# A fourth mask buffer, two residual buffers loaded later, and the first batch's input in halves

## The chip, the cores and the metric

The kernel runs on one core of one Trainium2 chip. The metric is the device time of one execution in microseconds (us). The time before is the median of seven runs, 2154.57 us (2151.7 to 2155.99). One execution was recorded by the hardware profiler; all readings of the profile are from that one, and times in it count from the start of its span.

The engines have short names in the profile: PE is TensorE (its matmuls; PEld its loads of weights), DVE is VectorE, ACT is ScalarE, POOL is GpSimd, and SP is SyncE, whose queue (SPq) issues most of the transfers.

## What is computed

One layer of a network on 32 graphs (batches) of 512 nodes with 256 features each, all in float32. Cut to what matters:

```python
h = relu(layernorm(x))                        # x: (32, 512, 256), over the features
xc = h.transpose(0, 2, 1)
c = relu(bn1(conv1d(xc, conv1_w)))            # one tap
c = bn2(conv1d(c, conv2_w, pad=8))            # 17 taps along the nodes
x_conv = relu(c + xc).transpose(0, 2, 1)
s = h @ w_se.T + b_se                         # three numbers per node
A = exp(-squared_distances(s)) * adj          # adj: (32, 512, 512), the mask
x_nmp = A @ relu(h @ w_msg.T + b_msg)
# a GRU cell, input [x_conv, x_nmp], state h
gi = concat(x_conv, x_nmp) @ w_ih.T + b_ih
gh = h @ w_hh.T + b_hh
r, z = sigmoid(gi_r + gh_r), sigmoid(gi_z + gh_z)
n = tanh(gi_n + r * gh_n)
out = x + (1 - z) * n + z * h                 # x: the layer's input, the residual
```

## The kernel before

**Streams.** Five streams of work are written as Python generators (line 1068): `rows` (layer norm and transposition of the first four batches, and the one-tap convolution of all), `begins` (the same preparation of the later batches), `graphs` (messages, distances, masking and the sum over neighbours), `conv` (the 17-tap convolution, four batches at a time, as 25 products of transformed inputs and transformed weights), and `gates` (the GRU cell and the output). A loop (line 1106) always takes the next piece of the stream that is furthest behind.

**A planner with a clock of its own.** The order of each engine's instructions is fixed while the program is built. `now` is an estimated time of PE, and every `matmul` or `turn` (a transposition on PE) adds to it. `Engine` (line 107) keeps an estimated `free` time for DVE and ACT: a fixed cost per instruction plus one per element. A generator yields the time from which its next piece may go. After each piece `fill` (line 1027) puts background work on DVE as long as `dve.free < now + 1.5`: layer norms of later batches (`norm_some`), the convolution's operands, transformed weights and sums. `later` (line 144) keeps short follow-up pieces until their time has come. So where a step yields, and what the estimate of `dve.free` is, can alter the written order of everything behind it.

**Layer norm.** `fetch` (line 161) loads 512 x 256 numbers as one transfer into a tile of 128 partitions by four chunks. `norm` (line 274) is a generator. For each chunk DVE makes statistics and aggregates them, and it yields after every second chunk; then `rsqrt` (line 212) adds epsilon on DVE and raises to the power -0.5 on POOL for all four chunks at once; then DVE makes the shifts, and ACT applies scale and shift to each chunk in place. For batch 0 the whole generator is run at once before the loop (line 1080), since nothing else can be done yet. PE then transposes the normed chunks (`norm_t`, line 309), and `conv1` (line 321) follows.

**Masks.** The 512 x 512 mask of a batch is four tiles of 128 rows, `m_sb`, with three buffers. `masked` (line 741) takes one tile: for the first eight batches PE transposes it into a PSUM bank (`ps_g`, of which there are three) and DVE multiplies it into `at`; for the others DVE transposes and multiplies. Then `gr.ask(1)` asks for one mask more. As the buffers are given out in turn, that is the mask three places on: the first three masks of a batch are asked for while the batch before is masked, and the fourth when the first of its own batch has been used. `gather` (line 756) then multiplies `at` with the messages.

**Residual.** At the end of a gate half (`o` is 0 or 1, half of the features), `leave` (line 911) transposes the result on DVE and adds `XR[b, o]`, the tile `res` with the layer's input in blocks of 32 x 32; `store` (line 918) writes it out from POOL's queue in four transfers. `load_res` (line 776) issues four transfers of 64 KB on SP's queue. `res` has three buffers. The two tiles of batch 0 are loaded after the first update of batch 0 (line 973), each later one when the tile of the same half of the batch before has been stored (line 928), two half-batches ahead.

**Gates.** `gates` (line 861) goes for each `o` through the products of r, of the hidden part, of z and of n. Their evacuations are `reset` (a sigmoid on ACT into `r`; before it `settle` writes out all pieces still kept by `later`, the store of the half before among them), `reset_hidden`, `update` (a sigmoid on ACT into `z`) and `mix`.

**When the gates start.** `late_pools` (line 686) opens the memory of the late stage when the first group's last product comes; there `whh` and `wih`, the GRU's weights (768 and 1536 KB), are loaded on SP's queue.

SP issues its transfers strictly in the written order; each waits for its buffer, and those behind it wait too.

Of the kernel before, what the change touches and what calls it, by code (L numbers as in the profile page):

```python
# [8 lines left out]
F32 = mybir.dt.float32  # L9
AF = mybir.ActivationFunctionType  # L10
ALU = mybir.AluOpType
PSUM = bass.MemoryType.PSUM

P = 128
# [21 lines left out]
TURNED = 8  # L36
# [8 lines left out]
def kernel(  # L45
# [28 lines left out]
    nc = tc.nc  # L74
    B, N, D = x.shape
    NT = N // P
    ND = D // P
# [8 lines left out]
    front = ctx.enter_context(tc.tile_pool(name="front", bufs=2))  # L86
# [7 lines left out]
    late = None  # L94
# [4 lines left out]
    LAG = 0.6  # L99
# [22 lines left out]
    dve, act = Engine(nc.vector, 0.12, 0.00108), Engine(nc.scalar, 0.16, 0.0009)  # L122
# [21 lines left out]
    def later(t, f):  # L144
        LATER.append((t, f))
        LATER.sort(key=lambda e: e[0])

    def settle():
        while LATER:
            LATER.pop(0)[1]()  # L150


    XS, HT, HB, HR, HG, XN, XR = {}, {}, {}, {}, {}, {}, {}
# [6 lines left out]

    def fetch(b, xs=None):
        XS[b] = front.tile([P, NT, D], F32, name="x_sb", bufs=2) if xs is None else xs
        nc.sync.dma_start(XS[b], x[b].rearrange("(c p) d -> p c d", p=P))

    def load(b, xs=None):
        if b not in XS:
# [13 lines left out]
    def load_gates(b):  # L180
        if b >= B or b in HB:
            return
        HB[b] = late.tile([P, ND, N], F32, name="hTb", bufs=2)
        nc.sync.dma_start(HB[b], HD[b])

    def load_sums(b, d):
        if b < B and (b, d) not in XN:
            XN[b, d] = late.tile([P, N], F32, name="xnb", bufs=2)
            nc.sync.dma_start(XN[b, d], ND_[b, d])
# [22 lines left out]
    def rsqrt(dst, var):  # L212

        n = dst.shape[-1]
        t = front.tile([P, 4], F32, name="veps")
        dve.tensor_scalar(t[:, :n], var, EPS, None, op0=ALU.add)
        nc.gpsimd.tensor_tensor(dst, t[:, :n], mhalf[:, :n], op=ALU.pow)
# [19 lines left out]
    class Graphs:  # L237
# [15 lines left out]
        def ask(self, more):  # L253

            for k in range(self.asked, min(self.asked + more, NT * B)):
                b, c = k // NT, k % NT
                m = self.masks[b, c] = front.tile([P, N], F32, name="m_sb", bufs=3)
                rows = adj[b].rearrange("(k i) m -> i k m", i=32)  # L260
                if b < TURNED:
                    nc.sync.dma_start(m, adj[b, c * P : (c + 1) * P, :])
                for g in range(P // 32 if b >= TURNED else 0):
                    at = c * P + 32 * g
                    nc.sync.dma_start(
                        m[32 * g : 32 * g + 32, :].rearrange("i (k j) -> i k j", j=32),
                        rows[:, :, at : at + 32],
                    )
                self.asked = k + 1

    gr = Graphs()


    def norm(b):

        xs = XS[b]
        st = front.tile([P, NT, 6], F32, name="st")
        mv = front.tile([P, NT, 2], F32, name="mv")
        for c in range(NT):
            dve.bn_stats(st[:, c, :], xs[:, c, :])  # L280
            dve.bn_aggr(mv[:, c, :], st[:, c, :])
            if c % 2:
                yield 0.0
        rstd = front.tile([P, NT], F32, name="rstd")
        rsqrt(rstd, mv[:, :, 1])
        yield dve.free + 2.0
        shift = front.tile([P, NT], F32, name="shift")
        dve.scalar_tensor_tensor(
            shift, mv[:, :, 0], -1.0, rstd, op0=ALU.mult, op1=ALU.mult
        )  # L290
        yield dve.free + 0.2
        for c in range(NT):
            act.activation(
                xs[:, c, :], xs[:, c, :], AF.Identity if b < TURNED else AF.Relu, bias=shift[:, c : c + 1],
                scale=rstd[:, c : c + 1],
            )
            if c % 2:
                yield act.free + LAG

    def norm_some(b):  # L300

# [284 lines left out]
    def all_operands():  # L586
        for _ in range(NG):
            yield from operands()

    xs = all_operands()  # L590
# [177 lines left out]
    def blocks(t, rows, o):  # L768
        for g in range(P // 32):
            at = o * P + 32 * g  # L770
            nc.sync.dma_start(
                t[32 * g : 32 * g + 32, :].rearrange("i (k j) -> i k j", j=32),
                rows[:, :, at : at + 32],
            )

    def load_res(b, o):
        if b < B and (b, o) not in XR:
            XR[b, o] = late.tile([P, N], F32, name="res", bufs=3)
            blocks(XR[b, o], XB[b], o)


# [79 lines left out]
    def gates(b):  # L861
# [33 lines left out]
        def mix_next(r, z, o, s):  # L895
            act.activation(
                r[:, s], r[:, s], AF.Tanh,
                bias=vec[:, _COL["b_ih"] + 2 * ND + o : _COL["b_ih"] + 2 * ND + o + 1],
            )
            later(act.free + 0.3, lambda: mix_last(r, z, o, s))  # L900
# [17 lines left out]
        def store(y, o, s):  # L918
            for g in range(P // 32):
                at = slice(32 * g, 32 * g + 32)  # L920
                queue = nc.gpsimd if s.stop - s.start == N else nc.scalar if g % 2 else nc.sync
                queue.dma_start(  # L922
                    OB[b][:, s.start // 32 : s.stop // 32, o * P + 32 * g : o * P + 32 * g + 32],
                    y[at, s].rearrange("i (k j) -> i k j", j=32),
                )
            if s.stop == N:
                del XR[b, o]
                load_res(b + 1, o)

        for o in range(ND):  # L930
            r = z = None

            def reset():
                nonlocal r
                settle()
                r = late.tile([P, N], F32, name="r", bufs=2)
                act.activation(r, ps_r, AF.Sigmoid, bias=brz[:, o : o + 1])

            def reset_hidden():
                dve.scalar_tensor_tensor(  # L940
                    r, ps_h, vec[:, _COL["b_hh"] + 2 * ND + o : _COL["b_hh"] + 2 * ND + o + 1], r,
                    op0=ALU.add, op1=ALU.mult,
                )

            def update():
                nonlocal z
                z = late.tile([P, N], F32, name="z")
                act.activation(z, ps_z, AF.Sigmoid, bias=brz[:, ND + o : ND + o + 1])

            def mix(s=slice(0, N)):  # L950
                dve.tensor_tensor(r[:, s], ps_n[:, s], r[:, s], op=ALU.add)
                later(dve.free + 0.3, lambda r=r, z=z, o=o: mix_next(r, z, o, s))
                if o == ND - 1:
                    load_sums(b + 1, 0)
                    load_sums(b + 1, 1)

            ps_r = acc.tile([P, N], F32, name="ps_acc")
            if o == 0:
                yield lambda: b in evacuated
                yield evacuated[b]  # L960
                yield from residual()
                yield from products(ps_r, o, 0, 0, 1, (0, 2))
                yield act.free + LAG
            else:
                yield from products(ps_r, o, 0, 0, 1, (0, 2))
            yield from products(ps_r, o, 0, 1, 3, (0, 2), reset)
            ps_h = acc.tile([P, N], F32, name="ps_acc")
            yield from products(ps_h, o, 2, 0, 1, (0, 0), reset_hidden)
            ps_z = acc.tile([P, N], F32, name="ps_acc")
            yield from products(ps_z, o, 1, 0, 3, (0, 2), update)  # L970
            if o == 0:
                load_gates(b + 1)
                for k in range(ND if b == 0 else 0):
                    load_res(0, k)
            ps_n = acc.tile([P, N], F32, name="ps_acc")
            if b < B - 1 or o < ND - 1:
                yield from products(ps_n, o, 2, 1, 3, (1, 2), mix)
                continue

            for h in range(2):  # L980
                s = slice(h * N // 2, (h + 1) * N // 2)
                if h > 0:
                    ps_n = acc.tile([P, N], F32, name="ps_acc")
                for j in range(2 * ND):
                    matmul(
                        ps_n[:, s], wih[:, j, cols(o, 2)], x_in[j][:, s],
                        start=(j == 0), stop=(j == 2 * ND - 1),
                    )
                mix(s)
                yield now  # L990
            settle()
# [109 lines left out]
    for c in range(ND):  # L1101
        for k0, k1 in ((0, 9), (9, TAPS)):
            nc.sync.dma_start(wflat[:, c, k0 + 1 : k1 + 1, :], conv2_w[:, c, k0:k1, :])
    gr.ask(3)

    while streams:
        names = [k for k in streams if hold[k] is None or hold[k]()]
# [6 lines left out]
        name = min(able, key=lambda k: clock[k])  # L1114
# [63 lines left out]
```

## Time and profile before

| what | before |
|---|---|
| median of seven runs | 2154.57 us |
| the profiled execution | 2154.1 us |
| its span | 2152.0 us |
| PE busy | 2095.2 us, 97% of the span |
| DVE busy | 1523.3 us, 71% |
| ACT busy | 763.3 us, 35% |
| moved by DMA | 367.11 MB, mean 171 GB/s |
| masks on SP's queue | 384 transfers of 64 KB, 32 of 256 KB |
| residual on SP's queue | 256 transfers of 64 KB |

The execution's own time is 2.1 us longer than its span. In a list of waits a line says which engine waited with which instruction, for whom, how many us in all, how often, and the longest in us. In a timeline a line starts with the start and the length in us; then come engine, line, operation, `out<-in`, how many such instructions are merged, and in brackets how long the engine had been idle before and what ended that. A line of an SPq row says when transfers were issued, not when they landed. The line of most instructions is that of a helper (118, 127, 132), so they are told apart by their tiles. The ends of matmuls are modelled, so a busy PE is not a PE at its peak.

### The profile page before, as it was taken

How to read it: one execution, taken by the hardware profiler on the slowest of the kernel's cores; microseconds unless marked ns; L12 is line 12 of the kernel's file. 1: busy time of each engine (PE TensorE's matmuls, PEld its weight loads, DVE VectorE, ACT ScalarE, POOL GpSimd, SP SyncE). 2: the span in 40 equal slices, each digit the busy share in tenths (PEclk: the TensorE clock that was granted, in tenths of full speed). 3: DMA queues.
4: the chain of work that ended last, by engine and by line, in shares of the span. 5: the costliest groups of instructions: out<-in, count | busy, mean ns of one | idle time of the engine just before them, and what ended most of it. 6: DMA issues, size and time to landing. Idle time of an engine off the chain costs nothing.

```text
span 2152.0 us, 26534 instructions
## 1 busy us (share of the span) xinstructions
PE 2095.2 (97%) x9200; PEld 1299.0 (60%) x9200; DVE 1523.3 (71%) x2818; ACT 763.3 (35%) x1277; POOL 296.8 (14%) x445
## 2 busy tenths in 40 slices
PE   7998999999999999999999999999999999999998
PEld 4875575566665666656665666656665566665443
DVE  6897688677776777667875777767777677776333
ACT  5635422433233342234324153243523324222311
POOL 2101112111111111111111111110111010011111
PEclk9999999999999999999999999999999999999999
DMA  7446576757676667765776766666675565554331
GB/s 271 166 167 227 172 207 191 204 171 193 150 209 175 178 177 199 201 187 148 197 183 197 206 151 190 194 170 187 179 193 150 152 162 143 142 166 92 70 74 34
DMA packets 539461, 367.11 MB, mean 171 GB/s; under 512 B 455232, under 2 KB 472000, under 8 KB 538688
## 3 DMA queue, kind: packets, MB, share of 16 engines
q1 hardware_dynamic: 511392, 282.95, 49.3%
q0 software_dynamic: 23248, 69.23, 10.1%
q10 hardware_dynamic: 4688, 13.24, 1.6%
q8 instruction: 73, 1.20, 0.2%
q14 instruction: 60, 0.49, 0.1%
HBM read 282.74 MB, written 82.58 MB: 170 GB/s over the span
## 4 chain that ended last, share of the span: by engine, by line
PE 83%; ACT 1%; DVE 1%; issue 0%; DVEq 0%; ACTq 0%
PE ps_acc L127 44%; PE ps_g L127 17%; PE ps_c L127 14%; PE ps_b L127 7%; PE ps_b L733 1%; PE ps_g L132 1%; ACT at L118 0%; DVE xconv L118 0%; ACT xconv L118 0%; ACT L118 0%; DVE r L118 0%; DVE o_sb L118 0%; PE ps_g L733 0%; DVE msg L118 0%; DVE res L118 0%
## 5 line engine op out<-in xcount | busy, mean ns | idle before, releaser
L127 PE MATMUL ps_acc<-xconv,wih 128*128 128x512 f32 (+1 forms) x772 | 362.8, 592 | 5.2 <-ACT xconv L118 5.2
L127 PE MATMUL ps_acc<-xnb,wih 128*128 128x512 f32 (+1 forms) x772 | 362.7, 592 | 0.0
L127 PE MATMUL ps_acc<-hTb,whh 128*128 128x512 f32 x768 | 355.9, 594 | 0.1
L127 PE MATMUL ps_c<-xd,w 128*128 128x116 f32 x2800 | 345.6, 277 | 4.3 <-DVE z L118 4.3
L127 PEld LDWEIGHTS ps_c<-xd,w 128*128 128x128 f32 x2800 | 331.3, 194 | 7.5 <-DVE z L118 4.6
L922 POOL DMA_DIRECT2D out_dram<-res x252 | 164.8, 660 | 942.8 <-DVE res L118 805.8
L118 DVE TENSOR_TENSOR r<-ps_acc,r 128x512 f32<-128x512 f32 (+1 forms) x65 | 44.4, 684 | 314.1 <-PE ps_acc L127 314.0
L127 PEld LDWEIGHTS ps_acc<-xnb,wih 128*128 128x128 f32 x772 | 141.9, 189 | 165.0 <-issue 163.3
L127 PEld LDWEIGHTS ps_acc<-xconv,wih 128*128 128x128 f32 x772 | 141.7, 190 | 157.3 <-issue 146.0
L127 PEld LDWEIGHTS ps_acc<-hTb,whh 128*128 128x128 f32 x768 | 141.8, 190 | 148.2 <-issue 144.0
L127 PE MATMUL ps_g<-at,msg 128*128 128x512 f32 x512 | 228.3, 597 | 2.9 <-DVE at L118 2.9
L127 PEld LDWEIGHTS ps_b<-x,w 128*128 128x128 f32 x1400 | 182.0, 191 | 71.1 <-issue 55.8
L118 ACT ACTIVATE mid<-ps_b 128x232 f32<-128x232 f32 x175 | 63.9, 365 | 370.2 <-PE ps_b L127 335.6
L127 PE MATMUL ps_b<-x,w 128*128 128x116 f32 x1400 | 183.3, 274 | 5.3 <-ACT at L118 5.3
L127 PEld LDWEIGHTS ps_g<-at,msg 128*128 128x128 f32 x512 | 96.7, 191 | 119.7 <-issue 113.1
L118 DVE SCALAR_TENSOR_TENSOR x<-x,x 128x480 f32<-128x480 f32 (+1 forms) x184 | 144.0, 783 | 3.0
L118 DVE TENSOR_TENSOR x<-x 128x240 f32<-128x240 f32 (+1 forms) x320 | 134.4, 462 | 0.5
L127 PE MATMUL ps_g<-wmsg,hTg 128*128 128x259 f32 x496 | 124.4, 382 | 0.7 <-ACT hT L118 0.7
L118 ACT ACTIVATE z<-ps_acc,brz 128x512 f32<-128x512 f32 x64 | 44.0, 687 | 220.5 <-PE ps_acc L127 220.3
L127 PE MATMUL ps_g<-hT,w 128*128 128x512 f32 x256 | 119.5, 611 | 1.2 <-ACT at L118 1.2
L127 PEld LDWEIGHTS ps_g<-wmsg,hTg 128*128 128x128 f32 x496 | 92.5, 190 | 44.2 <-issue 32.6
L118 DVE TENSOR_TENSOR xd<-x 128x480 f32<-128x480 f32 x175 | 113.2, 649 | 3.3 <-PE ps_c L127 3.3
(109 smaller groups left out, 2483.5 us busy)
## 6 DMA issues: line engine op xcount, KB each, us to landing
w<-wd SPq DMA_DIRECT2D x150, 768.0 KB, 5.9
m_sb<-in_adj_dram SPq DMA_DIRECT2D x384, 64.0 KB, 2.7
hd<-hT POOLq DMA_DIRECT2D x32, 512.0 KB, 6.1
hTb<-hd SPq DMA_DIRECT2D x32, 512.0 KB, 6.2
xnb<-nd SPq DMA_DIRECT2D x64, 256.0 KB, 3.2
res<-in_x_dram SPq DMA_DIRECT2D x256, 64.0 KB, 4.5
out_dram<-res POOLq DMA_DIRECT2D x252, 64.0 KB, 3.2
hTg<-hd SPq DMA_DIRECT2D x31, 512.0 KB, 4.5
```

The costliest lines, as they stand in the source:

```text
L118: getattr(self.engine, name)(*tiles, **more)
L127: nc.tensor.matmul(ps, lhsT, rhs, **more)
L132: nc.tensor.transpose(ps, a, ident)
L733: nc.tensor.matmul(pss[c], gr.left[k, :], gr.right[k, :], start=True, stop=True, tile_position=(32 * c, 0),)
L922: queue.dma_start(OB[b][:, s.start // 32 : s.stop // 32, o * P + 32 * g : o * P + 32 * g + 32], y[at, s].rearrange("i (k j) -> i k j", j=32),)
```

## The change

Four things are changed.

- Masks: the tile `m_sb` gets four buffers, and four masks, not three, are asked for before the loop.
- Residual: `res` goes from three buffers to two. The first tile is loaded in `reset` of batch 0, half 0. Every other one is loaded in `update` of the half-batch before it: in half 0 the other half of the same batch, in half 1 the first half of the next batch. The loads after a store and after the first update go.
- Batch 0's input: `fetch` issues two transfers of two chunks each, not one of four. The other batches keep one.
- Layer norm: for batch 0 `rsqrt`, shift and application go by halves of two chunks. For the other batches the operations are the same, but `rsqrt` is issued in the same step as the last statistics, where it was a step of its own.

```diff
     def fetch(b, xs=None):
         XS[b] = front.tile([P, NT, D], F32, name="x_sb", bufs=2) if xs is None else xs
-        nc.sync.dma_start(XS[b], x[b].rearrange("(c p) d -> p c d", p=P))
+        step = NT // 2 if b == 0 else NT
+        for c in range(0, NT, step):
+            nc.sync.dma_start(
+                XS[b][:, c : c + step], x[b].rearrange("(c p) d -> p c d", p=P)[:, c : c + step]
+            )
...
-                m = self.masks[b, c] = front.tile([P, N], F32, name="m_sb", bufs=3)
+                m = self.masks[b, c] = front.tile([P, N], F32, name="m_sb", bufs=4)
...
+        rstd = front.tile([P, NT], F32, name="rstd")
+        shift = front.tile([P, NT], F32, name="shift")
+        step = NT // 2 if b == 0 else NT
         for c in range(NT):
             dve.bn_stats(st[:, c, :], xs[:, c, :])
             dve.bn_aggr(mv[:, c, :], st[:, c, :])
+            if (c + 1) % step == 0:
+                rsqrt(rstd[:, c + 1 - step : c + 1], mv[:, c + 1 - step : c + 1, 1])
             if c % 2:
-                yield 0.0
-        rstd = front.tile([P, NT], F32, name="rstd")
-        rsqrt(rstd, mv[:, :, 1])
-        yield dve.free + 2.0
-        shift = front.tile([P, NT], F32, name="shift")
-        dve.scalar_tensor_tensor(
-            shift, mv[:, :, 0], -1.0, rstd, op0=ALU.mult, op1=ALU.mult
-        )
-        yield dve.free + 0.2
-        for c in range(NT):
-            act.activation(
-                xs[:, c, :], xs[:, c, :], AF.Identity if b < TURNED else AF.Relu, bias=shift[:, c : c + 1],
-                scale=rstd[:, c : c + 1],
+                yield dve.free + 2.0 if c == NT - 1 else 0.0
+        for c0 in range(0, NT, step):
+            k = slice(c0, c0 + step)
+            dve.scalar_tensor_tensor(
+                shift[:, k], mv[:, k, 0], -1.0, rstd[:, k], op0=ALU.mult, op1=ALU.mult
             )
-            if c % 2:
-                yield act.free + LAG
+            yield dve.free + 0.2
+            for c in range(c0, c0 + step):
+                act.activation(
+                    xs[:, c, :], xs[:, c, :], AF.Identity if b < TURNED else AF.Relu,
+                    bias=shift[:, c : c + 1], scale=rstd[:, c : c + 1],
+                )
+                if c % 2:
+                    yield act.free + LAG
...
-            XR[b, o] = late.tile([P, N], F32, name="res", bufs=3)
+            XR[b, o] = late.tile([P, N], F32, name="res", bufs=2)
...
                 del XR[b, o]
-                load_res(b + 1, o)
...
                 settle()
+                if b == o == 0:
+                    load_res(b, o)
                 r = late.tile([P, N], F32, name="r", bufs=2)
...
                 nonlocal z
+                load_res(b + o, 1 - o)
                 z = late.tile([P, N], F32, name="z")
...
                 load_gates(b + 1)
-                for k in range(ND if b == 0 else 0):
-                    load_res(0, k)
...
-    gr.ask(3)
+    gr.ask(4)
```

## The prediction

> **What bounds the kernel now.** I read the page first: engine shares, then the chain.
>
> ```profile
> PE 2095.2 (97%) x9200; PEld 1299.0 (60%) x9200; DVE 1523.3 (71%) x2818; ACT 763.3 (35%) x1277; POOL 296.8 (14%) x445
> ...
> PE 83%; ACT 1%; DVE 1%; issue 0%; DVEq 0%; ACTq 0%
> ```
>
> TensorE (PE) is busy for 97% of the span and holds the chain, and the change removes no matmul. It can gain only where PE stands still: 2152.0 - 2095.2 = 56.8 us. The second view is who PE waited for, whole run:
>
> ```profile
> PE ps_g L132 <- DMA m_sb<-in_adj_dram: 9.7, 1, 9.7
> PE ps_g L132 <- ACT x_sb L118: 9.3, 1, 9.3
> PE ps_b L127 <- ACT at L118: 5.3, 6, 1.6
> PE ps_acc L127 <- ACT xconv L118: 5.2, 4, 1.3
> ```
>
> One late mask and the wait for the first normed batch are 19.0 of the 56.8 us; no other single wait is over 2.3 us. The change touches both. Third, the timeline of PE around the late mask, with DVE's and SP's for the same time:
>
> ```profile
> 205.60 1.04 PE L132 MATMUL ps_g<-ident,m_sb 128*128 128x128 f32 x8
> 207.13 0.66 PE L132 MATMUL ps_g<-ident,m_sb 128*128 128x128 f32 x4 [0.49 <-ACT h L118]
> 217.46 1.09 PE L132 MATMUL ps_g<-ident,m_sb 128*128 128x128 f32 x4 [9.67 <-DMA m_sb<-in_adj_dram]
> ```
>
> ```profile
> 209.99 0.68 DVE L118 TENSOR_TENSOR at<-ps_g,at 128x512 f32<-128x512 f32 x1
> 210.59 1.60 DVE L118 TENSOR_TENSOR y<-y,z 128x1392 f32<-128x1392 f32 x1
> 212.10 1.28 DVE L118 TENSOR_TENSOR at<-ps_g,at 128x512 f32<-128x512 f32 x2
> 218.58 0.69 DVE L118 TENSOR_TENSOR at<-ps_g,at 128x512 f32<-128x512 f32 x1 [5.20 <-PE ps_g L132]
> ```
>
> ```profile
> 200.73 0.42 SPq L693 DMA_DIRECT2D wih<-in_w_ih_dram  x1
> ...
> 206.23 1.91 SPq L262 DMA_DIRECT2D m_sb<-in_adj_dram  x2
> ```
>
> Three masks were there. The fourth was only asked for at 206.2, when the first had been read, and so queued behind the GRU weights; it landed at 217.3.
>
> **What the skill says.** The Trainium skill, "DMA: Bandwidth & Descriptors", Specifications, puts HBM at about 358 GB/s per core; the trace agrees (362 GB/s, share 0.94, over 197 to 217 us), so the burst can't be hurried and only an earlier place in it helps. The same page, Anatomy of one DMA, gives about 2 us fixed per transfer, mostly the receipt (for the software path); here the first 512 KB of x, issued at 0.75, had its last packet at 4.07 and released VectorE (DVE) at 4.75. "TensorE: Matmul & The Clock Gate", Part 1, says that an idle window of about 3.4 us halves PE's clock and a busy one restores it. The trace agrees: the granted clock was 0.50 over 217 to 223 us, and 1.00 after.
>
> **Part 1, fourth mask buffer.** Each consumed mask asks for the mask four on, not three on. The fourth mask of this graph is then asked for while the previous graph is masked, and its SP requests stood at 145.7 to 156.6: 50 us early. The DMA wait becomes 0. What is late next is a PSUM bank. The three ps_g banks hold masks 0 to 2, and the first comes free when DVE ends its first product, 209.99 + 0.68 = 210.7. The transposes then end at about 210.7 + 1.09 = 211.8. DVE is at its next products until 212.10 + 1.28 = 213.4, makes the fourth (0.69) by 214.1, and the gather starts then, not at 219.33: **5.2 us**. Of PE's 9.67 + 0.78 us of idle time about 5.2 stays, owed to DVE's sums. The gate still closes in it. Before, the gather ran at half clock from 219.33 to 223.0, a loss of 1.84 us; re-warming from a random phase takes one to two windows, 3.4 to 6.8 us, so loses 1.7 to 3.4, in the mean 2.55. That takes 0.7 back: **-4.5 us**; bounds -3.6, and -7.0 if PE stays warm. The next work is ready: the hT row asked for at 204.61 needed 12.0 us (landing 216.6), and PE wants it some 4 to 5 us after 214.1, with 2 us to spare.
>
> At the start four masks are asked for, not three: 256 KB more, 0.7 us at 362 GB/s, landing 15 us after their issue at 11 us; the first is used at 36.5. Hidden; without that cover 0.7 us. In the other graphs no mask wait stands in PE's list, so I count nothing for them.
>
> **Part 2, halves for batch 0.** The first lines of the timeline:
>
> ```profile
> 4.75 0.43 DVE L118 BATCH_NORM_STATS2 st<-x_sb 128x6 f32<-128x256 f32 x1 [4.75 <-DMA x_sb<-in_x_dram]
> ...
> 7.33 1.04 POOL L217 TENSOR_TENSOR rstd<-veps,mhalf 128x4 f32<-128x4 f32 x1 [4.46 <-DVE veps L118]
> 8.41 0.16 DVE L118 SCALAR_TENSOR_TENSOR shift<-mv,rstd 128x4 f32<-128x4 f32 x1 [1.23 <-POOL rstd L217]
> ...
> 8.61 2.07 ACT L118 ACTIVATE x_sb<-x_sb,shift,rstd 128x256 f32<-128x256 f32 x4 [2.52 <-DVE shift L118]
> ```
>
> In the trace's packets the 256th of the 512 was done at 3.39, 0.68 us before the last; with the same tail the first half lands at 4.07. Two stats and aggregates take 1.17 (4.75 to 5.92): 5.24. The first veps takes 0.1 of DVE's time, so the second pair ends at about 6.49 and its veps at 6.70. The first pow on POOL starts 0.32 after its veps and takes 0.70 for two columns (the bn_rs row): 5.57 to 6.27. The first shift stands behind the second veps in DVE's order: 6.72. ScalarE (ACT) starts 0.20 later, at 6.92, not 8.61: **-1.7 us**. The second pow runs 6.85 to 7.55, its shift at 7.6, before ACT ends its first two at 8.0, so the four activations stay unbroken. Added: a DMA issue (0.5 us on SP), a veps (0.17), a pow (0.70), a shift (0.16); the last three are in this sum. The SP issue pushes vec, conv1_w and the rest back by up to 0.5; vec landed at 6.4 and is now wanted at 7.7, conv1_w (7.6) before PE wants it at about 10.1. The first weights' sums start at 25.7 on data landed at 16.5 and 19.8, so 1.7 us earlier is covered. From there on PE and ACT stand in one chain (ACT 9.1 of 10 us busy over 20 to 30), so I pass all of it on. Bounds: 0 (absorbed) to -2.1.
>
> **Part 3, the norm's steps of other batches.** The pow joins the second pair of stats: one planner step fewer per batch, and the planner's DVE clock 0.24 us higher after batch 0 (two more instructions at 0.12). No work is added, but the written order of DVE's background work may differ. PE's waits of 0.6 to 2.3 us between 9 and 205 us sum to 11, and those from 240 to 2000 us to another 11; a new order redraws them. Central value 0, bounds -4 and +4.
>
> **Part 4, the residual.** 256 requests before and after. A load for half-batch k+1 is now placed at the update of k, into the buffer of k-1. From the trace I compared each store's landing with the z activation of the next half-batch: it came 1.4 us (k = 30 and 58) to 26 us earlier, so SP is never held beyond the update. The load is used at the soonest 15 + 8 us later (last batches: one half-batch, then from z to the last addition) and lands in 4 to 10. Behind it on SP stand hTb, xnb, masks and weights, none sooner wanted. Cost 0; -0.5 to +2.
>
> **Sum.** -4.5 - 1.7 + 0 + 0 = -6.2 against the profiled execution: 2154.1 - 6.2 = 2147.9 (its span 2152.0 to 2145.8, 2.1 us around it). The median shown is 0.5 higher, so 2148.4.
>
> **Rivals.** *The gains meet other waits.* If the start is absorbed, or the new order costs 2 to 5 us, what is left is 2150.3 to 2154. For it: PE and DVE share the load until 205 us (DVE 19.7 of 20 at 100 to 120). Against: PE's list shows no DMA wait there. *The new order also removes small waits.* If it saves some of the 22 us of Part 3, 3 to 8 us more: 2140.5 to 2145.5. Nothing in the profile points that way rather than the other. *The burst hits hT instead* (slower). At 204 to 217 us everything queues at 362 GB/s. If the new order puts that row, or the first weights, behind the four masks, conv1's rows wait where the mask did. It has 2 us to spare; each us beyond that costs one. At 6.2 + 4.3 + 2, landing 12.5 us later than 216.6, the kernel is slower by 0.2%: about 2160. Against: the row is asked for before the masks, and a whole 1 MB of masks is only 2.9 us. *The change doesn't take effect*: no, four buffers and halves are static.
>
> **How the numbers follow.** A measurement of this kernel tells some 0.2%, 4.3 us, so faster means below 2150.3. Both gains arrive: 0.62, own range 2145 to 2151, a tenth of it over the bound. Gains absorbed: 0.18, mostly same. More removed: 0.10. Slower rival: 0.10. Faster 0.56 + 0.03 + 0.10 = 0.69; same 0.06 + 0.14 + 0.01 = 0.21; slower 0.10. Range 2142 to 2155: it leaves out half of the third case and the fourth, and a little of the first two.
>
> **What would show it.** The first activation at 6.9 and first transpose near 7.6 us; no mask in PE's list of waits, and near 205 us an idle time of 2 to 3 us on DVE's products twice; res loads in fours at each update; DVE never waiting for res. The prediction is wrong if PE's list holds a new wait over 3 us, or if more half-clock windows appear before 240 us.

## The result and the profile after

| | before | after |
|---|---|---|
| median | 2154.42 us | 2149.08 us |
| ratio, with its 95% interval | | 0.9975 (0.9968 to 0.9982) |
| the profiled execution | 2154.1 us | 2146.66 us |
| its span | 2152.0 us | 2144.8 us |
| PE busy | 2095.2 us | 2089.9 us |

The change makes the kernel faster by 0.25%: 5.4 us (3.9 to 6.9) of 2154.4, where 6.2 were forecast. The profiled execution gained more, 7.4 us; the last part of the explanation says why.

The page of the changed kernel, engine shares and chain:

```profile
PE 2089.9 (97%) x9200; PEld 1293.7 (60%) x9200; DVE 1526.3 (71%) x2820; ACT 762.2 (36%) x1277; POOL 299.7 (14%) x446
...
PE 83%; ACT 1%; DVE 1%; issue 0%; DVEq 0%; ACTq 0%
```

PE still carries the chain; nothing took its place. Who PE waited for, over the whole run (total us, times, longest):

```profile
PE ps_g L132 <- ACT x_sb L118: 7.2, 2, 7.0
...
PE ps_c L127 <- DVE z L118: 5.4, 2, 3.2
...
PE ps_g L127 <- DVE at L118: 4.9, 3, 2.7
PE ps_g L132 <- DVE at L118: 3.4, 2, 2.9
PE ps_c L127 <- DVE x L118: 2.7, 1, 2.7
```

The mask's line is gone from the list, the first wait fell from 9.3 to 7.0, and two waits of 2.9 and 2.7 us for DVE's masked products (`at`) are new. So is one of 2.7 us for the convolution's operand `x`, near 150 us, and the longest wait for `z`, another operand, has grown from 2.2 to 3.2 us. The timeline of PE and then of DVE around the fourth mask (start, length; in brackets the idle time before):

```profile
203.29 0.66 PE L132 MATMUL ps_g<-ident,m_sb 128*128 128x128 f32 x4 [0.49 <-ACT h L118]
206.88 0.66 PE L132 MATMUL ps_g<-ident,m_sb 128*128 128x128 f32 x4 [2.93 <-DVE at L118]
210.19 6.18 PE L127 MATMUL ps_g<-at,msg 128*128 128x512 f32 x8 [2.65 <-DVE at L118]
```

```profile
206.14 0.68 DVE L118 TENSOR_TENSOR at<-ps_g,at 128x512 f32<-128x512 f32 x1
206.74 1.60 DVE L118 TENSOR_TENSOR y<-y,z 128x1392 f32<-128x1392 f32 x1
208.26 1.88 DVE L118 TENSOR_TENSOR at<-ps_g,at 128x512 f32<-128x512 f32 x3
```

The fourth mask is there. Its transposition starts when DVE has ended the first product (206.14 + 0.68) and so freed a bank, and the gather starts when the three others are done. 2.93 + 2.65 us of the 10.45 stay. The start of the run:

```profile
3.59 0.43 DVE L118 BATCH_NORM_STATS2 st<-x_sb 128x6 f32<-128x256 f32 x1 [3.59 <-DMA x_sb<-in_x_dram]
...
6.34 2.08 ACT L118 ACTIVATE x_sb<-x_sb,shift,rstd 128x256 f32<-128x256 f32 x4 [1.42 <-DVE shift L118]
```

The first half is there 1.16 us sooner, ACT starts 2.27 us sooner, and its four activations are one row. The other 1.11 us come from the norm in halves; the two halvings were not run apart.

### The profile page after: what moved, and what is told of

Its sections match the earlier page's. It is cut to its first block, busy times and chain, and to the rows that moved or that the text cites. A ratio compares the mean times of both kernels' runs of the same rounds, so it can differ in the third digit from the quotient of the medians.

```text
span 2144.8 us, 26566 instructions
## 1 busy us (share of the span) xinstructions
PE 2089.9 (97%) x9200; PEld 1293.7 (60%) x9200; DVE 1526.3 (71%) x2820; ACT 762.2 (36%) x1277; POOL 299.7 (14%) x446
## 4 chain that ended last, share of the span: by engine, by line
PE 83%; ACT 1%; DVE 1%; issue 0%; DVEq 0%; ACTq 0%
PE ps_acc L127 44%; PE ps_g L127 17%; PE ps_c L127 14%; PE ps_b L127 7%; PE ps_b L740 1%; PE ps_g L132 1%; ACT at L118 0%; DVE xconv L118 0%; ACT xconv L118 0%; ACT L118 0%; DVE r L118 0%; DVE o_sb L118 0%; PE ps_g L740 0%; DVE msg L118 0%; DVE res L118 0%
```

## The experiments

All were timed against the kernel before on the same chip. "From the ratio" means the ratio's distance from 1 times 2154.6 us; the interval is the 95% one.

### The buffers alone

The masks' and the residual's parts of the change in the kernel before. The written order of PE, DVE, ACT and POOL is unchanged, line for line; only SP's differs.

```diff
-                m = self.masks[b, c] = front.tile([P, N], F32, name="m_sb", bufs=3)
+                m = self.masks[b, c] = front.tile([P, N], F32, name="m_sb", bufs=4)
...
-            XR[b, o] = late.tile([P, N], F32, name="res", bufs=3)
+            XR[b, o] = late.tile([P, N], F32, name="res", bufs=2)
...
-    gr.ask(3)
+    gr.ask(4)
```

> Four mask buffers and two residual buffers with their later loads, in the kernel before; layer norm, halves and the written order of PE, DVE, ACT and POOL as before. My theory (the late mask was the cost): PE's wait for the mask of 9.7 us becomes two idle times of 2.9 and 2.3 to 2.7 us that DVE ends, the gather starts 5 us earlier, and the time falls by 4.5 us (3.6 to 7.0). Rival (the gain of the changed kernel came from the new written order): under 1 us. Rival (the residual's loads cost something that other gains covered): under 3 us, with waits of DVE for res.

Measured: 2151.91 us, ratio 0.9984 (0.9977 to 0.9991): -3.4 us (-1.9 to -5.0). PE's timeline:

```profile
211.08 1.12 PE L132 MATMUL ps_g<-ident,m_sb 128*128 128x128 f32 x4 [2.94 <-DVE at L118]
214.39 6.70 PE L127 MATMUL ps_g<-at,msg 128*128 128x512 f32 x8 [2.19 <-DVE at L118]
```

Nearly as expected: 2.94 and 2.19 us stay. With the same order each instruction can be set against its twin in the kernel before: just before the masks it ran 0.4 us late, at the gather 4.9 early, at 240 us 3.7 early. So the wait is worth 5.3 us, and the half clock after it (a stretch in which the profile has a granted clock of 0.50) takes back 1.2: 4.1. In this trace a half-clock window at 323 us, which the twin's has not, then takes 1.7 more. The masks' rival (a gain of the new order alone) falls.

A tile of either kind is 512 numbers, 2 KB of each partition, and the memory plan has no room for four masks beside three residual tiles (the late stage then lacks 1.75 KB). Making that room is what the residual's change is worth here.

### The weights behind the mask

In the kernel before, the GRU's weights are issued after the first mask request that follows the opening of the late stage.

```diff
         whh = late.tile([P, ND, 3 * D], F32, name="whh")
         wih = late.tile([P, 2 * ND, 3 * D], F32, name="wih")
-        nc.sync.dma_start(whh, w_hh)
-        nc.sync.dma_start(wih, w_ih)
...
             gr.ask(1)
+            ask_gru()
             return
```

> The kernel before, with its three mask buffers, but the two transfers of the GRU's weights (2.3 MB) are issued behind the request for the fourth mask, not ahead of it. If the mask was late because it stood behind the weights, its landing moves from 217 to about 210 us, PE waits under 2 us for it, and the time falls by 3.5 to 4.5 us without any buffer more. If asking for it at its first neighbour's use was too late in any case (the rest of the burst is 3 MB), PE still waits 5 us or more and the gain is under 2 us.

Measured: 2150.34 us, ratio 0.9974 (0.9962 to 0.9986): -5.6 us (-3.0 to -8.2).

```profile
212.99 1.08 PE L132 MATMUL ps_g<-ident,m_sb 128*128 128x128 f32 x4 [4.52 <-DVE y L118]
214.86 6.74 PE L127 MATMUL ps_g<-at,msg 128*128 128x512 f32 x8 [0.78 <-DVE at L118]
```

The view puts the end of the 4.52 us down to DVE's sum `y`, which ended near by and which the transposes don't read; by the trace's landings it was the mask. It landed at 212.86, not at 217.32, so PE's wait fell from 9.7 to 4.5 us and not, as I had expected, to under 2: when the mask was issued at 206.92, 2 MB of the burst (the transfers issued from 197 us on) still stood ahead of it. But a mask that is there in time starts the gather at 214.39 (the run above), and this one at 214.86, since DVE's sums take most of those 4.5 us anyhow: DVE ended the first product, and so freed a bank, only at 211.34, 2.9 us into the wait. So it was the place in the queue that made the mask late, and a deeper buffer is one cure of two.

### Batch 0 in halves alone

`fetch` and `norm` as changed for batch 0 only, and the planner's DVE clock set back by the 0.24 us of the two added instructions; every other instruction keeps its place.

```diff
-        NORMS[b] = norm(b)
+        NORMS[b] = norm(b) if b else norm_first(b)
...
+    dve.free -= 0.24
     bn1_sc, bn1_sh = bn_affine("bn1")
```

> Batch 0's input and norm in halves, with the planner's estimates set so that the order of everything else stays as before; three mask and three residual buffers. My theory (PE and ACT stand in one chain from the start): first activation at 6.3 us (as in the changed kernel's trace), first transposition at 7.0, and all 2.3 us are still there at 200 us and at the end: -2.3 us. Rival (absorbed by the shared load of PE and DVE before 205 us): under 0.7 us.

Measured: 2151.71 us, ratio 0.9987 (0.9980 to 0.9993): -2.8 us (-1.5 to -4.3). First transposition at 6.91. Against its twin the run is 2.0 us early at 42 to 94 us, only 0.3 early at 160 (a half-clock window at 98.6 us is its own), and 1.9 to 2.0 early again at 240 to 580 (the kernel before has one of its own at 188.9). The gain isn't absorbed.

### The order alone

The changed kernel's `norm`, but whole for batch 0 as well, in the kernel before; the 0.24 us are added to the planner's clock by hand, so that the written order is that of the changed kernel. The first two lines below are set against the changed kernel's `norm`, the last against the kernel before.

```diff
-        step = NT // 2 if b == 0 else NT
+        step = NT
...
+    dve.free += 0.24
     bn1_sc, bn1_sh = bn_affine("bn1")
```

> Only the written order of the changed kernel (the norm's steps merged, the planner's DVE clock 0.24 us higher), with batch 0 whole and three mask and three residual buffers. My theory: 0 +- 2 us; the late mask's wait of about 9 us and the first wait of 9.3 us stand as before. Rival (the new order brings gains of its own, since at 157 to 205 us the changed kernel gained 1.6 us more): -1.5 to -3 us. A new wait of 2.7 us at about 150 us (DVE's operand x) should be there too.

Measured: 2155.15 us, ratio 0.9998 (0.9990 to 1.0006): -0.4 us (-2.2 to +1.3). The mask's wait is 9.01 us, the first 9.27. The wait of 2.7 us near 150 us, which I had put down to the order, is not there, so that part of the expectation was wrong; the residual's run below has it with the old order. The three parts add up: 3.4 + 2.8 + 0.4 = 6.6, inside the interval of the whole change (3.9 to 6.9).

The order isn't idle, though. The longer wait for `z` comes with it; PE in the kernel before, in this one and in the changed kernel:

```profile
326.03 2.04 PE L127 MATMUL ps_c<-xd,w 128*128 128x116 f32 x16 [2.06 <-DVE z L118]
```

```profile
326.20 3.61 PE L127 MATMUL ps_c<-xd,w 128*128 128x116 f32 x16 [2.94 <-DVE z L118]
```

```profile
317.86 3.54 PE L127 MATMUL ps_c<-xd,w 128*128 128x116 f32 x16 [3.19 <-DVE z L118]
```

With the new order a wait of 0.67 us stands 4 us ahead of it and a half-clock window follows it, and this run loses 3.2 us on the kernel before between 300 and 420 us. It wins back 1.6 us each at 738 and 1428 us, where the kernel before has half-clock windows and this one has none. So the order's zero is a sum of a loss and of gains; whether the missing windows are owed to the order isn't shown.

### The residual alone

```diff
-            XR[b, o] = late.tile([P, N], F32, name="res", bufs=3)
+            XR[b, o] = late.tile([P, N], F32, name="res", bufs=2)
...
                 nonlocal z
+                load_res(b + o, 1 - o)
```

> Only the residual: two buffers, each load at the update of the half-batch before; three mask buffers, order of PE, DVE, ACT and POOL as before. My theory: 0 (-0.5 to +2 us), DVE never waits for res, and the late mask's wait stands at about 9 us. Rival (holding SP's queue at the store's landing costs, and the buffers run together would have gained the full 4.5 us of the mask without it): +1 us or more, with new waits of PE or DVE for w, hT or xnb after 250 us.

Measured: 2154.24 us, ratio 1.0000 (0.9992 to 1.0008). What SP's queue waited for, in the kernel before and then in this one:

```profile
SPq L771 <- DMA out_dram<-res: 20.8, 9, 6.1
```

```profile
SPq L771 <- DMA out_dram<-res: 186.4, 49, 13.9
```

SP is held nine times as long for stores to land, and nobody pays: DVE's additions never wait for `res`, the ratio is 1, and the late mask's wait is 9.2 us, as long as in the runs with the old loads (9.0 to 9.7). A queue that issues in order may be held as long as nothing behind it is wanted sooner.

### The sums held back

This and all runs below go past the change. In the changed kernel, DVE's sums of the convolution are kept from the distances of a batch to its last masking while the first group's last products are out.

```diff
     def sum_some():
-        if not SUMS:
+        if not SUMS or (masking and at_product == 25):
             return False
...
+        masking = True
         kernel_exp(at)
         yield act.free + 0.3
         for n in range(NT):
             masked(b, at, n)
             if n < NT - 1:
                 yield dve.free - 0.2
+        masking = False
```

> The changed kernel, but from a batch's distances to its last masking DVE's sums of the convolution are held back while the first group's last products are out. If the two idle times of PE left at 204 to 210 us (2.93 and 2.65 us) are owed to those sums on DVE, the four masked products run in one row, the fourth mask is transposed straight after the third, the gather starts about 5 us sooner than in the changed kernel, and the clock gate may stay open: -3 to -6 us more. Rival (the held sums make the first residual, and so the gates, late): the gain shows at 205 us and is given back before 260 us.

Measured: 2145.34 us, ratio 0.9954 (0.9941 to 0.9966): -9.9 us against the kernel before, 4.5 more than the change.

```profile
204.89 1.09 PE L132 MATMUL ps_g<-ident,m_sb 128*128 128x128 f32 x8 [0.40 <-DVE at L118]
206.92 3.70 PE L127 MATMUL ps_g<-at,msg 128*128 128x512 f32 x8 [0.94 <-DVE at L118]
214.14 2.68 PE L127 MATMUL ps_g<-hT,w 128*128 128x512 f32 x3 [3.52 <-DMA hT<-hd]
```

The two idle times shrink to 0.40 and 0.94 us, so they were owed to the sums; the gather runs at full clock (3.70 us for eight, where it was 6.18). And at once the next thing is late: the row of `hT`, which stands in the same burst.

> The same hold on the changed kernel's buffers and halves, but with the planner's estimates up to there as in the kernel before. It tells the hold's effect from the order that happens to follow it: if the hold is what counts, its gain over the changed kernel is within 2 us of that of the other hold.

With the order of the kernel before up to there: 2146.42 us, ratio 0.9962 (0.9949 to 0.9974): -8.2 us. Within 2 us of the other, so it is the hold that counts.

### PE warmed at the start

In the changed kernel PE multiplies the identity with itself twelve times while it would wait for the first batch; nothing reads the result.

```diff
     make_identity(nc, ident)
+    ps_w = acc.tile([P, N], F32, name="ps_acc")
+    for _ in range(12):
+        nc.tensor.matmul(ps_w[:, :P], ident, ident, start=True, stop=True)
```

> The changed kernel with twelve products of the identity with itself on PE from about 2 us on, while PE has nothing to do; their result isn't used. If the clock gate's slow start costs time after 7 us (the first eight one-tap products took 5.1 us at the start and 3.6 to 3.7 later), PE reaches full clock before 9.6 us and everything behind comes 0.7 to 1.5 us sooner. If PE isn't what the first 20 us hang on (ACT is), it gains under 0.4 us; if the products run past 7 us, it loses by as much.

Measured: 2146.35 us, ratio 0.9962 (0.9949 to 0.9974), 2.8 us beyond the change's own ratio, with intervals that meet. The first one-tap products take 3.70 us where the changed kernel has 5.76, and the transposition of `augr` behind them starts at 19.48, not 21.30. Whether this reaches the end is not settled: see the last run.

### Sums held, weights behind, and all three

The hold on the changed kernel, with the weights issued behind the first mask request, as above.

> The changed kernel with the held sums and, besides, the GRU's weights issued behind the first mask request of that graph. With the sums held PE met a new wait of 3.5 us for the hT row, which stood behind the weights in the same burst. If the burst's order is what makes it late, the row lands by about 207 us, that wait goes, and the time falls 2 to 3.5 us below the held kernel's, to about 2142. If the next wait (the aug factors, or the weights themselves before the first gate) takes its place, it falls by under 1 us.

Measured: 2137.87 us, ratio 0.9922 (0.9908 to 0.9936): -16.8 us (-13.8 to -19.8). The gather and the row behind it:

```profile
204.74 3.70 PE L127 MATMUL ps_g<-at,msg 128*128 128x512 f32 x8 [0.94 <-DVE at L118]
208.28 3.60 PE L127 MATMUL ps_g<-hT,w 128*128 128x512 f32 x8
```

No wait is left between them. The gain over the held kernel is 6.9 us, twice what I expected. The two traces account for it, one of each: besides the 3.5 us, a half-clock window that began with that wait (214.4) and a wait of 2.3 us at 245 us (0.7 now) with another such window (245.1) are gone, and one window (222.4) is new: 3.5 + 1.7 + 1.6 + 1.7 - 1.7 = 6.8.

> The same and the twelve idle-time products on PE at the start. If the three are independent, the start's 2 to 2.7 us come on top: about 2139.5 to 2140, 14 to 15 us below the kernel before.

2138.30 us, ratio 0.9926 (0.9913 to 0.9939): the warm start adds nothing here, against the expectation. In the traces it is 1.4 us ahead at 20 us and not ahead at 185, where the two kernels' same waits end at 185.31 and 185.37; this trace has half-clock windows at 63 and 97 us, the other has not. One trace of each doesn't tell chance from rule, so the warm start's worth stays open.

> The same on the planner's order of the kernel before up to the hold. If the order between 9 and 200 us is worth nothing, within 1.5 us of the other.

2138.46 us, ratio 0.9925 (0.9912 to 0.9938): within 1.5 us, as expected.

The best version is the changed kernel with the sums held and the weights behind the mask: 2137.87 us, 0.78% below the kernel before, where the change alone has 0.25%. The last two runs can't be told from it, and it is the simplest of the three.

## Why the prediction was right

**The mask.** The step held: the wait of 9.67 + 0.78 us became two idle times on DVE's products, 2.93 + 2.65 in the changed kernel and 2.94 + 2.19 with the order of before, where the prediction's times give 2.9 and 2.3. The saving was 5.3 us by the trace of the buffers' run (5.2 forecast). What the clock takes back depends on where its windows fall. Counted from the gather's start, the half clock lasted 3.7 us in the kernel before, 5.0 in the changed kernel (to 215.2) and 6.1 in the buffers' run (to 220.5); that costs 1.84, 2.5 and 3.1 us. So 0.7 went back in the changed kernel, as forecast, and 1.2 in the buffers' run. Both stretches lie within the one to two windows that the prediction estimated from the Trainium skill's page "TensorE: Matmul & The Clock Gate", Part 1. The changed kernel and the order's run have all 9200 matmuls in the same order: the changed kernel is 4.1 us ahead of it before the masks and 8.6 after them, a gain of 4.5, the forecast's figure. By the clock on the wall the buffers were worth 3.4 us (1.9 to 5.0). One reading went too far: the burst's 362 GB/s isn't shown to be a limit, since the same trace has 369 and 370 GB/s over 10 to 20 and 20 to 30 us, above the 358 that the prediction quotes.

**The start.** The mechanism held, and the size was too small: 1.7 forecast, 2.3 at the first activation, 2.8 (1.5 to 4.3) at the end. The mis-sized term is the first half's landing: 4.07 by the sum, 3.59 measured. The sum took the 256th packet's end from the one big transfer (3.39) and added its 0.68 us to release. As a transfer of its own the half had its last packet at 3.04 and released DVE 0.55 later. That it passes on to the end was right: in the halves' run 1.9 to 2.0 us of 2.3 are there from 20 to 94 us and again from 240 us on.

**The order and the residual.** Both were taken at 0 and measured -0.4 (-2.2 to +1.3) and 0.0 (-1.7 to +1.7). That a new order redraws the small waits was right, and they do not cancel in every stretch, as the order's run shows. The prediction also said that SP is never held beyond the update. SP waits for stores for 186 us in all, but it comes to its requests early: in the residual's run the store that it waits for had always landed by 1.8 us before the sigmoid of that update.

**The sum.** Mask and start came out 1.1 us under and 1.1 us over their forecasts, each forecast inside the measured interval. That 3.4 and 2.8 make 6.2 again is luck; the whole change has 5.4.

**The rivals.** Neither gain was absorbed. The row of `hT` was the right thing to fear, but its slack was mis-sized: 2 us were forecast, and in the buffers' run it landed at 216.02 and PE came to it at 220.93, 4.9 us later, as the gather ran at half clock; in the changed kernel it was 3.9 us. In the held kernel, which came to it earlier, it was 3.5 us late.

**The signs of being wrong.** One came in part: a wait over 3 us is in PE's list, the one of 3.19 us for `z`, grown from 2.06. It belongs to the order (2.94 in the run of the order alone), which the prediction took at 0 within 4 us. The other did not come: before 240 us the changed kernel's profiled run was at half clock for 13.6 us, that of the kernel before for 30.7.

**Profiled run and median.** The profiled run gained 7.4 us, the medians 5.3. Half-clock windows are part of it: before its last products the profiled run of the kernel before was at half clock for 41 us, that of the changed kernel for 20.5, and a window of 3.4 us full of work costs 1.7. Some 2 us of this is chance: the held kernel has the same matmuls in the same order up to 226 us, and at 190 its trace is 1.7 us later, with windows at 64, 98, 136 and 187 us where the changed kernel's has one, at 150. Over all runs the granted clock was nearly the same (mean 0.9907 in 15 runs of the changed kernel, 0.9902 in 46 of the kernel before). A difference of 0.0005 over 2150 us is 1.1 us at most, so the medians are the better measure.

## What to carry to other kernels

When one transfer is late, look at what stands ahead of it in its queue: asking earlier (a deeper buffer) and letting the big, less urgent transfer go behind it started the same gather within 0.5 us of each other, and the second needs no memory. Before counting a wait as gain, name what is late next and its slack: here a bank held up by DVE's sums, then a row with a few us to spare, and taking each in its turn brought three times the gain of the first. Where PE's clock falls during a wait, a difference of 2 us between single traces can be chance; set twins of the same written order side by side.

## What the runs showed of the hardware that was not expected

Half a transfer was earlier than half of it: split in two, 256 of the 1 KB packets were done at 3.04 us, where the 256th of the undivided transfer was done at 3.39, with the same issue at 0.75. It is so in every trace looked at: 2.96 to 3.04 in the three with halves (the changed kernel, the halves alone, PE warmed), 3.39 to 3.43 in the four without (the kernel before, the buffers, the weights, the residual). Why isn't shown.

The half-clock windows of 3.4 us fall in other places from run to run with one written order. The wait for DVE's `z` near 325 us is 2.06 us in the kernel before and has no such window; in the buffers' run it is 2.16 us and has one, and in the residual's run 2.20 us and none. In the changed kernel's 15 runs the mean granted clock went from 0.989 to 0.994, and the time from 2151.7 to 2145.0 us.
